# Turning x in 32x32 blocks on VectorE from a second load, in place of on TensorE, in a two-layer graph kernel

## The chip, the cores and the metric

One core of one Trainium2 chip. The time is device microseconds (us) of one execution, at a granted TensorE clock of 0.995 to 0.997 in the profiled ones. Before: 3906.45 us, median of 4 runs (3906.17 to 3907.53); the execution that was profiled took 3903.31. Verdicts count from 2%.

## The reference, cut to what matters

```python
# x: (32, 512, 512) f32, adj: (512, 512) of 0 and 1, deg = adj.sum(axis=1)
mi = einsum('bkd,od->bko', x, Wi);  mj = einsum('bkd,od->bko', x, Wj)
h  = layernorm(x + deg * (mi + b) + einsum('ij,bjo->bio', adj, mj))   # layer 0
q, k, v = heads(h @ Wq.T + bq), heads(h @ Wk.T + bk), heads(h @ Wv.T + bv)   # 8 heads of 64
out = layernorm(h + (softmax(where(adj == 0, -inf, q k^T / 8)) @ v) @ Wo.T + bo)   # layer 1
```

The kernel's matmuls sum over the partitions of their operands, so layer 0 needs x turned (feature in the partition) times the degrees, called XD here, and the gathered neighbours adj x, called AX_T.

## The kernel before

A period works on three batches at once and is cut into eight attention steps. Each begins with scores and the values of the step before, followed by pieces of projections: `l0` (layer 0), `v`, `q`, `k` and `pj` (output projection). Each projection is computed in seven products by a Strassen-like scheme, so a piece is called q6, and GpSimd makes the differences that it needs (`combos`). The turn of x stood in the gather:

```python
def l0_gather(b, dc, bank, adjT=None):
    xt = XT[b]
    if dc == 0:
        XD[b] = big()
        AX_T[b] = big()
    pt = turn_tile()                                   # PSUM, of the scores' pool
    for jc in range(NC):
        nc.tensor.transpose(pt[:, jc*P:(jc+1)*P], xt[:, jc, dc*P:(dc+1)*P], ident)
    nc.vector.tensor_mul(XD[b][:, dc, :], pt, deg_r)
    pm = mm_tile(bank)
    ...                                                # adj x: 4 + 4 matmuls
    nc.scalar.copy(AX_T[b][:, dc, :], pm)
```

Which piece stands in which step is not written down: it follows from weights.

```python
STEPS = 2 * HP
PC, TR, GA = 1.73, 0.44, 1.9           # a piece, a turn, a gather
...
    g = [(TR + GA, l0_gather, n, dc, A) for dc in range(DC)]
...
def by_steps(todo):                     # equal shares of the summed weights
    total, done, at, res = sum(f[0] for f in todo), 0.0, 0, []
    for step in range(STEPS):
        res.append([])
        while at < len(todo) and (done < total * (step + 1) / STEPS - 1e-6 or step == STEPS - 1):
            res[-1].append(todo[at])
            done += todo[at][0]
            at += 1
    return res
```

## Time and profile before

| | before |
|---|---|
| time | 3906.45 us |
| TensorE busy | 3853.7 us, 99% |
| one period, first scores to first scores, mean of 27 | 120.06 us |
| first scores of the first period | 107.6 us |

The chain of waits, followed back from the last instruction:

```profile
PE 77%; DVE 12%; POOL 8%; issue 2%; ACT 1%; DMA 0%; SPq 0%
```

The chain passes through another engine wherever TensorE was released by it, however short the wait was.

### The profile page before, as it was taken

The numbers are of one execution on the slowest core, as the hardware profiler recorded it, in microseconds if no ns is written. First come the engines' busy times: TensorE is split into PE (matmuls) and PEld (weight loads), VectorE is DVE, ScalarE is ACT, GpSimd is POOL, SyncE is SP. The second block draws the span as 40 slices with busy tenths as digits, with TensorE's granted clock in tenths as the row PEclk, the third lists the DMA queues.
The fourth block names the chain that finished last, engine by engine and source line by source line (L and its number), as shares of the span: only waits on it lengthen the run. The fifth ranks groups of instructions, "written<-read, shape, count | busy, mean of one in ns | idle before, by whom it ended". The sixth has DMA issues, their size and how long they took to land.

```text
span 3901.5 us, 46958 instructions
## 1 busy us (share of the span) xinstructions
PE 3853.7 (99%) x17402; PEld 2641.4 (68%) x17402; DVE 2595.7 (67%) x3520; ACT 1057.0 (27%) x1476; POOL 1909.7 (49%) x1861
## 2 busy tenths in 40 slices
PE   9999999999999999999999999999999999999997
PEld 6666666766666666676666666666666667666663
DVE  4667676666666676666767666666667666676765
ACT  2222222222222222322222222222222232222222
POOL 4455544554544545445555455453454544555533
PEclk9999999999999999999999999999999999999998
DMA  7333333323334233343333343333433333333330
GB/s 251 116 108 100 114 108 116 120 92 110 115 108 124 87 116 111 111 119 108 99 115 108 116 119 92 109 116 108 124 87 116 111 111 119 108 99 115 108 108 23
DMA packets 281865, 433.87 MB, mean 111 GB/s; under 512 B 23072, under 2 KB 119840, under 8 KB 281632
## 3 DMA queue, kind: packets, MB, share of 16 engines
q1 hardware_dynamic: 281376, 430.27, 36.2%
q8 instruction: 142, 2.33, 0.2%
q14 instruction: 91, 0.75, 0.1%
q0 software_dynamic: 256, 0.53, 0.0%
HBM read 389.29 MB, written 41.42 MB: 110 GB/s over the span
## 4 chain that ended last, share of the span: by engine, by line
PE 77%; DVE 12%; POOL 8%; issue 2%; ACT 1%; DMA 0%; SPq 0%
PE mma L375 23%; PE mmb L375 23%; PE sc L427 10%; PE ov L448 9%; POOL xh L390 5%; PE mmb L299 3%; DVE rl L470 3%; PE mma L299 3%; PE ov L455 2%; DVE xh L393 2%; DVE st L265 2%; POOL big L344 2%; DVE e L432 2%; POOL es L438 2%; PE sc L292 2%
## 5 line engine op out<-in xcount | busy, mean ns | idle before, releaser
L432 DVE TENSOR_TENSOR e<-sc,edge 128x1024 f32<-128x1024 f32 x512 | 602.1, 1217 | 424.3 <-ACT sc L431 424.3
L431 ACT ACTIVATE sc<-sc 128x1024 f32<-128x1024 f32 x512 | 492.8, 1006 | 1271.3 <-PE sc L427 1271.1
L375 PE MATMUL mmb<-ring,big 128*128 128x256 f32 x3144 | 731.5, 381 | 3.4 <-POOL big L344 3.0
L375 PE MATMUL mma<-ring,big 128*128 128x256 f32 x3112 | 725.2, 381 | 4.2 <-POOL big L344 3.1
L375 PEld LDWEIGHTS mmb<-ring,big 128*128 128x128 f32 x3144 | 590.8, 190 | 124.1 <-DVE e L432 23.5
L375 PEld LDWEIGHTS mma<-ring,big 128*128 128x128 f32 x3112 | 583.9, 190 | 129.5 <-DVE e L432 25.2
L344 POOL TENSOR_TENSOR big<-big 128x512 f32<-128x512 f32 x376 | 549.8, 1489 | 220.1 <-DVE big L293 177.9
L184 POOL TENSOR_TENSOR xlo<-xh,xhi 128x512 fp32r<-128x512 f32 x128 | 203.1, 1597 | 735.1 <-ACT xhi L183 735.1
L427 PE MATMUL sc<-q,k 64*128 64x512 f32 x2048 | 509.5, 616 | 0.0
L448 PE MATMUL ov<-e,v 128*64 128x512 f32 x2048 | 496.0, 605 | 5.7 <-DVE oT L480 5.7
L470 DVE RECIPROCAL rl<-ov 128x128 f32<-128x128 f32 x512 | 462.6, 929 | 9.7 <-PE ov L465 5.5
L375 PE MATMUL mma<-big,ring 128*128 128x256 f32 x1808 | 433.1, 382 | 2.2 <-DVE xh L393 2.2
L375 PE MATMUL mmb<-big,ring 128*128 128x256 f32 x1776 | 425.3, 382 | 3.1 <-DVE xh L393 2.2
L267 POOL TENSOR_SCALAR mv<-mv 128x1 f32<-128x1 f32 x256 | 50.8, 198 | 735.5 <-DVE mv L266 724.1
L438 POOL TENSOR_TENSOR es<-e 128x1024 f32<-128x1024 f32 x128 | 301.4, 2355 | 198.6 <-PE ov L455 185.6
L375 PEld LDWEIGHTS mma<-big,ring 128*128 128x128 f32 x1808 | 337.9, 190 | 80.5 <-issue 26.0
L375 PEld LDWEIGHTS mmb<-big,ring 128*128 128x128 f32 x1776 | 332.0, 190 | 78.6 <-issue 24.3
L448 PEld LDWEIGHTS ov<-e,v 128*64 128x64 f32 x2048 | 124.5, 136 | 345.8 <-issue 270.9
L440 DVE TENSOR_TENSOR es<-es,e 128x1024 f32<-128x1024 f32 x248 | 341.6, 1377 | 0.0
L427 PEld LDWEIGHTS sc<-q,k 64*128 64x128 f32 x2048 | 176.5, 186 | 208.7 <-issue 208.2
L393 DVE TENSOR_TENSOR xh<-xh,mma 128x512 f32<-128x512 f32 x186 | 125.6, 676 | 213.1 <-PE mma L375 213.1
L393 DVE TENSOR_TENSOR xh<-xh,mmb 128x512 f32<-128x512 f32 x186 | 125.7, 676 | 203.6 <-PE mmb L375 202.5
(145 smaller groups left out, 3812.4 us busy)
## 6 DMA issues: line engine op xcount, KB each, us to landing
ring<-wq SPq DMA_DIRECT2D x160, 256.0 KB, 2.6
ring<-wv SPq DMA_DIRECT2D x160, 256.0 KB, 2.6
ring<-wk SPq DMA_DIRECT2D x160, 256.0 KB, 5.4
ring<-wi SPq DMA_DIRECT2D x155, 256.0 KB, 2.6
ring<-wj SPq DMA_DIRECT2D x155, 256.0 KB, 2.7
ring<-wo SPq DMA_DIRECT2D x155, 256.0 KB, 2.6
xh<-in_x_dram SPq DMA_DIRECT2D x32, 1024.0 KB, 6.0
out_dram<-xh SPq DMA_DIRECT2D x31, 1024.0 KB, 5.2
```

The costliest lines, as they stand in the source:

```text
L184: nc.gpsimd.tensor_sub(lo, xs, hi.bitcast(FT))
L299: nc.tensor.matmul(pm, parts[w][:, jc, :], adjR[:, jc, :], start=(w == 0 and jc == 0), stop=(w == 1 and jc == NC - 1))
L344: nc.gpsimd.tensor_tensor(dst, p, q, op=OP.subtract)
L375: nc.tensor.matmul(pm[:, c * Q:(c + 1) * Q], lhs, rhs, start=first, stop=(kc == 1 and n == len(terms) - 1), skip_group_check=True)
L393: nc.vector.tensor_tensor(d, d, pm, op=OP.add)
L427: nc.tensor.matmul(ps[:, s, :], KT[b, hp // 2][r, hp % 2, kc * P:(kc + 1) * P], QT[b, hp // 2][r, hp % 2, :], start=True, stop=True)
L431: nc.scalar.activation(ps, ps, AF.Exp, scale=QSCALE)
L432: nc.vector.tensor_tensor(e, ps, edge[:, kc:kc + 1, :].to_broadcast([P, 2, N]), op=OP.mult)
L438: nc.gpsimd.tensor_add(ES[hp], E[0], E[1])
L440: nc.vector.tensor_add(ES[hp], ES[hp], E[half])
L448: nc.tensor.matmul(PV[hp][s * HD:(s + 1) * HD, :], V[b][:, kc, c0:c0 + HD], E[kc][:, s, :], start=(kc == 0), stop=(kc == NC - 1))
L470: nc.vector.reciprocal(rl[:, c], pl[:, c])
```

## The change

Its intent: TensorE is the bound, so take work off it. From batch 1 on a second load puts 32x32 blocks of x where they belong after the turn, each block still unturned; VectorE turns the blocks, and GpSimd multiplies by the degrees. TensorE turns only h. The tile for the second load takes 8 KB per partition, and the ring of weights gives up four tiles for it. The core of the diff (cuts are marked `...`; `z(...)` puts work into the plan with weight 0):

```diff
+    def load_xa(b, q):
+        if q == 0:
+            XA[b] = work([P, DC, N], "xa", 1)
+        src = x[b].rearrange("(t p) (c q f) -> q p c t f", p=32, q=4, f=32)
+        nc.sync.dma_start(XA[b][32*q:32*q+32].rearrange("p c (t f) -> p c t f", f=32), src[q])
...
-    RING = 12
+    RING = 8
...   # l0_gather: the turn and its multiply only for a batch that is not in XA
+    def l0_turn(b, dc):
+        if dc == 0:
+            XD[b] = big()
+        nc.vector.transpose(XD[b][:, dc, :], XA[b][:, dc, :])
+        nc.gpsimd.tensor_tensor(XD[b][:, dc, :], XD[b][:, dc, :], deg_r, op=OP.mult)
...   # phase_a(n)
-        g = [(TR + GA, l0_gather, n, dc, A) for dc in range(DC)]
+        g = [(GA, l0_gather, n, dc, A) for dc in range(DC)]
             res += g[i:i + 1] + k[i:i + 1]
+            if n + 1 < B:
+                res += [z(load_xa, n + 1, i)]
...   # phase_c(n), after the pieces q6 and v6, q7 and v7, q4 and v4, q5 and v5
+            if n + 1 < B and i != 3:
+                res += [z(l0_turn, n + 1, (6, 7, 4, 5).index(i))]
```

Batch 1's second load stands at the start, between the load of x and that of the last weights.

More of the change, by code (lines that the diff above doesn't have):

```diff
@@ L96, in turn_tile @@
         return sc_tile()[:, 0, :]
-    XT, XD, AX_T, HT, MV = {}, {}, {}, {}, {}
+    XT, XA, XD, AX_T, HT, MV = {}, {}, {}, {}, {}, {}
     QT, KT, V, OT = {}, {}, {}, {}
@@ L103, in rows @@
         return ap.rearrange("(c p) d -> p c d", p=P)
+    def load_xa(b, q):
+        if q == 0:
+            XA[b] = work([P, DC, N], "xa", 1)
+        src = x[b].rearrange("(t p) (c q f) -> q p c t f", p=32, q=4, f=32)
+        nc.sync.dma_start(XA[b][32 * q:32 * q + 32].rearrange("p c (t f) -> p c t f", f=32), src[q])
     def load_x(b):
@@ L148, in gnn_attention_kernel @@
     load_x(1)
+    for q in range(4):
+        load_xa(1, q)
     wo = load_w(work([P, NC, D], "xh", 3), woT, nc.sync)
@@ L287, in l0_gather @@
         if dc == 0:
-            XD[b] = big()
+            if b not in XA:
+                XD[b] = big()
             AX_T[b] = big()
-        pt = turn_tile()
-        for jc in range(NC):
-            nc.tensor.transpose(pt[:, jc * P:(jc + 1) * P], xt[:, jc, dc * P:(dc + 1) * P], ident)
-        nc.vector.tensor_mul(XD[b][:, dc, :], pt, deg_r)
+        if b not in XA:
+            pt = turn_tile()
+            for jc in range(NC):
+                nc.tensor.transpose(pt[:, jc * P:(jc + 1) * P], xt[:, jc, dc * P:(dc + 1) * P], ident)
+            nc.vector.tensor_mul(XD[b][:, dc, :], pt, deg_r)
         pm = mm_tile(bank)
@@ L307, in l0_gather @@
             split(b, dc + 2)
+    def l0_turn(b, dc):
+        if dc == 0:
+            XD[b] = big()
+        nc.vector.transpose(XD[b][:, dc, :], XA[b][:, dc, :])
+        nc.gpsimd.tensor_tensor(XD[b][:, dc, :], XD[b][:, dc, :], deg_r, op=OP.mult)
     def base(b, half):
```

## The prediction

> **What bounds the kernel now.** I read the page's busy table first, then TensorE's own waits, then the turns of x one by one in the timeline.
>
> ```profile
> span 3901.5 us, 46958 instructions
> PE 3853.7 (99%) x17402; PEld 2641.4 (68%) x17402; DVE 2595.7 (67%) x3520; ACT 1057.0 (27%) x1476; POOL 1909.7 (49%) x1861
> ```
>
> TensorE is idle for 3901.5 - 3853.7 = 48 us in all, at a granted clock of 0.997. The ends of matmuls are modelled, so 99% alone proves little. The list of what TensorE waited for is the better witness:
>
> ```profile
> PE ov L448 <- DVE oT L480: 5.7, 4, 2.5
> ...
> PE mma L375 <- POOL big L344: 3.1, 14, 0.2
> PE mmb L375 <- POOL big L344: 3.0, 14, 0.2
> PE mma L375 <- DVE xh L393: 3.0, 15, 0.8
> PE mmb L375 <- DVE xh L393: 2.2, 14, 0.2
> ```
>
> (Us in total, times, longest.) All its waits come to 36 us, and the first of these lines and those left out stand almost wholly in the first 10 us or the last 165. In the 31 periods between it waits some 12 us. So in steady state the end is set by how much TensorE has to issue, and time comes off only where TensorE's own work goes, or is lost where another engine newly makes it wait. (The chain of waits gives VectorE 12% and GpSimd 8%; I don't take that as removable, since TensorE hardly idles for them.)
>
> Now the work to be removed, the turns of x:
>
> ```profile
> L292 PE MATMUL sc<-ident,xh x512: 272/273/331, 14.4 to 3684.6; 128*128 128x128 f32 x171
> ...
> 1142.40 0.60 PE L292 MATMUL sc<-ident,xh 128*128 128x128 f32 x4
> 1142.76 1.17 PE L299 MATMUL mma<-adjR,xhi 128*128 128x512 f32 x4
> ...
> 1163.15 0.66 PE L292 MATMUL sc<-ident,xh 128*128 128x128 f32 x4
> 1163.56 1.17 PE L299 MATMUL mma<-adjR,xhi 128*128 128x512 f32 x4
> ```
>
> One turn reads as 273 ns, and four as 0.60 us, but matmuls overlap: the next work starts 0.36 us after the first of four (1142.40 to 1142.76), or 0.41 us where the turn follows an attention matmul. The start to start time is what TensorE pays, not the printed 0.60.
>
> **What the Trainium skill says.**
> - "VectorE: DVE Perf Modes", section "The three transpose paths": VectorE turns only 32x32 blocks, each by itself, and takes 311 ns for 128x128 bf16. "Vector Engine (DVE) Microarchitecture Reference", section 3.8, has the turn sustain one element per cycle per lane. The kernel before has no such instruction; its 128x512 one-source conversion from PSUM took 0.69 us (L163). Scaling 311 ns by 384 more elements at 0.96 GHz (the first page's clock) gives 0.71 us. I take 0.70 as an estimate, 0.62 from start to start, as neighbours of that length show.
> - "SBUF — State Buffer", section "Who interferes with whom": a VectorE instruction with two SBUF inputs and a GpSimd one that reads SBUF block each other. The trace agrees: the sums of exponentials (L440, two SBUF inputs) take 1218 ns at the median and up to 2175.
> - "DMA: Bandwidth & Descriptors", section "Specifications": pieces under 512 B miss the line rate. The second load moves 128 B pieces. The trace has 48 such packets, at 13 to 44 ns each.
>
> **The change part by part.** A period (one batch) is 125 us, 31 of them lose their turns (batch 0 keeps its own).
>
> 1. *TensorE loses 31 x 4 groups of four turns.* In the period shown they cost 0.36 + 0.36 + 0.35 + 0.41 = 1.48 us. 31 x 1.48 = 45.9 us. This lies wholly on the bounding engine. Ideal result: 3906.7 - 45.9 = 3861.
>
> 2. *VectorE: multiply out of PSUM replaced by a turn in SBUF.* 124 x 0.68 us (L293) go, 124 x 0.70 come: about 0 in sum. But the work moves, from the gathers to between the last pieces of q and v. There VectorE's evictions have deadlines of one or two pieces (1.73 us each). The timeline of VectorE in that stretch, before:
>
> ```profile
> 1135.69 0.69 DVE L401 TENSOR_TENSOR v<-mmb,p 128x512 f32<-128x512 f32 x1 [1.24 <-PE mmb L375]
> 1136.30 1.22 DVE L440 TENSOR_TENSOR es<-es,e 128x1024 f32<-128x1024 f32 x1
> 1137.43 0.87 DVE L418 SCALAR_TENSOR_TENSOR q<-mma,bq_c,q 128x256 f32<-128x256 f32 x2
> 1138.22 1.51 DVE L440 TENSOR_TENSOR es<-es,e 128x1024 f32<-128x1024 f32 x1
> 1139.65 0.68 DVE L403 TENSOR_TENSOR v<-v,mmb 128x512 f32<-128x512 f32 x1
> 1140.88 0.88 DVE L418 SCALAR_TENSOR_TENSOR q<-mma,bq_c,q 128x256 f32<-128x256 f32 x2 [0.55 <-PE mma L375]
> ```
>
> No idle time for 4.6 us, and then only 0.55. The plan also drops 4 x 0.44 from a period's weights, so attention steps begin elsewhere. By the kernel's rule I get for the fifth step: scores, values, q4, v4, q5, v5, q3, v3 (before: v4, q5, v5, q3, v3 and a gather), with turns after the scores, after v4 and after v5. Counted from the step's start with the trace's durations: q4 leaves TensorE at 5.57 and is evicted by 6.53, the first sum of exponentials runs to 7.67, v4's eviction to 8.28, the second sum to 9.70, the turn to 10.33, and q5's eviction to about 11.2. TensorE wants that bank for q3 at 10.75. So about 0.45 us of new waiting in a period, 30 x 0.45 = 14 us. The other three turns fall on slack by the same counting.
>
> 3. *The moved steps give something back.* Before, the first step ends with a projection that waits for GpSimd's differences (the 3.1 + 3.0 us of such waits listed for banks a and b, about 0.2 us a period). Now scores and values come between. Minus 6 us.
>
> 4. *GpSimd gains 124 multiplies* of 128x512 with two SBUF inputs, the form of L344, median 1272 ns: 158 us, 49% to about 53% busy. It has the room, but block and be blocked by VectorE's two-input sums just in the tight stretch of point 2; I put 4 us on it. In exchange the differences of x need no longer wait for VectorE (178 us of GpSimd's idle time end with L293); that idle time costs TensorE nothing today, so I count nothing.
>
> 5. *DMA gains 1 MB a period in 8192 pieces.* At 16 to 44 ns on 16 engines that is 8192 / 16 x 16 to 44 ns = 8 to 23 us of DMA time, 2 to 6 us for each of the four loads. DMA is now 36% busy over a period, so about 43 to 55% after. Hidden, unless it holds up the weights.
>
> 6. *The ring of 8 in place of 12.* Weights now land far ahead:
>
> ```profile
> ring<-wq SPq DMA_DIRECT2D x160, 256.0 KB, 2.6
> xh<-in_x_dram SPq DMA_DIRECT2D x32, 1024.0 KB, 6.0
> ...
> SPq L486 <- ACT xh L272: 155.4, 31, 54.7
> ```
>
> I set every tile's landing against its first matmul: at least 17 us, median 26, are between. Four tiles less are some 10 us less; issuing each tile when the eighth before it is released, behind the same stores and loads of x in the queue, I get at least 8 us. So nothing is lost, if each new load keeps the queues for less than about 7 us (55 ns a packet).
>
> 7. *Start.* 1 MB more of small pieces stands ahead of the last weights; first needed at 53 us, they were issued at 15 us. I put 3 us on stores behind them.
>
> Sum: -45.9 + 14 - 6 + 4 + 3 = -31 us, 3876. I lean to the lighter side, since the waiting of point 2 hangs on a few tenths, and say **3871 us**, 0.9% less.
>
> **The rivals.**
> - *The whole 46 us arrive (3858 to 3862).* For it: TensorE hardly waits today, VectorE has a third of its time free, XD is ready much earlier. Against it: the tight stretch above. Perhaps three in ten.
> - *VectorE becomes the bound locally.* If the turn takes twice my estimate (1.4 us), the wait before q3 grows to about 1.2 us and others appear before v3 and v7: 1.5 us a period, the gain is cancelled, 3900 to 3910. For it: no 32-bit turn was measured here. One in ten.
> - *The ring starves.* If 128 B packets take over 55 ns, four loads of over 7 us run into a ring that lost a third of its depth. At 62 ns (8 us) the sum of the shortfalls is small, at 80 ns it would be 30 us or more a period at worst, and the kernel clearly slower, over 4000. For it: the skill's warning on pieces under 512 B. Against it: 15 ns is the commonest of the trace's few 128 B packets, and 1 KB takes 46. Under one in ten.
> - *The gain is larger than the turns' own time.* It would need TensorE to have other waits worth taking; the list has too few. 2% is 78 us; the turns and the waits of the periods together are 46 + 12 = 58.
>
> **Range and chances.** 3855 is all of point 1 and 3 with nothing lost; 3893 is 14 us left of the gain. Faster by over 2% (under 3829) 0.02, within 2% 0.93, slower by over 2% 0.05, nearly all of it from the ring.
>
> **What would show it.** TensorE's busy time should fall by about 45 us with its turns of x at 16 (batch 0); VectorE's turns should read about 0.7 us; GpSimd should be near 53%; a wait of TensorE on VectorE's evictions of q (about 0.45 us before q3, some 14 us in all) should appear and the wait on GpSimd's differences should go. Tiles of the ring should wait for their loads nowhere. Wrong would be: TensorE waiting for DMA, loads of the second copy landing after 8 us or more, a turn well over 1 us, or a time under 3850 (then TensorE paid more for a turn than starts show).

## The result, and the profile after

The changed kernel took **3837.43 us** (median of 4, 3835.97 to 3838.15): 69 us less. The ratio is 0.9822, 95% interval 0.9805 to 0.9839. Ratios are the mean time of one kernel's fast runs over that of the other's of the same rounds, so not quite the ratio of the medians. The prediction was wrong: 3871 was said and 3855 was its low end, and the gain of 69 us is nearly twice the 36 forecast.

The page and its chain of waits, after:

```profile
span 3835.8 us, 46277 instructions
PE 3794.4 (99%) x16906; PEld 2595.5 (68%) x16906; DVE 2587.3 (67%) x3520; ACT 1064.0 (28%) x1476; POOL 1990.0 (52%) x1985
...
q1 hardware_dynamic: 537312, 462.78, 41.7%
...
PE 92%; DVE 5%; ACT 1%; DMA 1%; issue 1%; POOL 0%; SPq 0%; POOLq 0%; DVEq 0%; ACTq 0%
```

TensorE's busy time fell by 59 us, not by the 46 of the turns. GpSimd left the chain (8% to 0%) although it works more. DMA engines are 42% busy in place of 36%. TensorE's waits after (line waited for, us in total, times, longest):

```profile
PE ov L466 <- DVE oT L498: 5.8, 5, 2.5
PE sc L169 <- DVE big L163: 5.4, 3, 4.0
...
PE mma L393 <- ACT p L400: 3.0, 1, 3.0
PE mma L310 <- POOL xlo L193: 1.5, 1, 1.5
PE mma L393 <- DVE v L419: 1.1, 2, 0.6
```

Nothing that recurs every period is left in the list, and no load is in it. What the moved work costs, by its own lines (shortest, median and longest in ns; first start to last end in us). VectorE's turn:

```profile
L324 DVE STREAM_TRANSPOSE big<-xa x124: 651/702/707, 76.2 to 3597.5; 128x512 f32<-128x512 f32 x124
```

GpSimd's multiply:

```profile
L325 POOL TENSOR_TENSOR big<-big,deg_r x124: 1261/1269/1282, 77.1 to 3598.2; 128x512 f32<-128x512 f32 x124
```

The second load, among the page's DMA issues (KB each, median us from issue to landing):

```profile
xa<-in_x_dram SPq DMA_DIRECT2D x124, 256.0 KB, 3.8
```

Turn 702 ns, multiply 1269 ns, load 3.8 us from issue to landing, all near the estimates. The error is elsewhere. To find it I measured every piece of work on TensorE from its first matmul's start to the start of what follows, and averaged over 28 periods of each kernel. These sums are mine, from the records of the trace; a period went from 120.05 to 117.65 us:

| place in the period | before | after | difference |
|---|---|---|---|
| four groups of turns of x | 1.48 | 0 | -1.48 |
| pj2 (second product of the output projection) | 2.12 | 1.78 | -0.34 |
| l06 and pj6 (with the wait at pj6) | 5.76 | 5.38 | -0.38 |
| gathers and pieces beside them: g0, k6, g1, k7, g2, g3 | 11.36 | 11.05 | -0.31 |
| v5 and q3 (with the wait at q3) | 3.50 | 3.75 | +0.26 |
| the rest, mostly borders of steps | | | -0.15 |

A piece without a wait takes 1.73 us, one of `l0` 3.46. Much of what counts stands in the list of waits in part or not at all, for that list counts idle time only from the modelled end of the matmul before. At pj6 it had 0.21 us; from start to start l06 took 3.83 us in place of 3.46. TensorE at that place before, then after (start, busy time from first to last, engine, line, operation, output and inputs, forms, count, and in brackets the idle time before it):

```profile
1062.43 2.29 PE L375 MATMUL mma<-ring,oT 128*128 128x256 f32 x8
1064.56 3.62 PE L375 MATMUL mmb<-ring,big 128*128 128x256 f32 x16
1068.39 1.99 PE L375 MATMUL mma<-ring,big 128*128 128x256 f32 x8 [0.21 <-POOL big L344]
1070.32 1.99 PE L427 MATMUL sc<-q,k 64*128 64x512 f32 x8
```

```profile
1050.48 1.94 PE L393 MATMUL mma<-ring,oT 128*128 128x256 f32 x8
1052.25 3.62 PE L393 MATMUL mmb<-ring,big 128*128 128x256 f32 x16
1055.80 1.99 PE L445 MATMUL sc<-q,k 64*128 64x512 f32 x8
1057.72 1.94 PE L466 MATMUL ov<-e,v 128*64 128x512 f32 x8
1059.58 2.00 PE L393 MATMUL mma<-ring,big 128*128 128x256 f32 x8
```

Compare starts. pj2 (first line) lasted 2.13 and now 1.77 us, without any wait being printed in either. l06 lasted 3.83 before pj6 could begin; after, scores and values (`sc`, `ov`) come between.

### The profile page after: what moved, and what is told of

The parts are those of the page before. It is cut to its first block, busy times and chain, and to the rows that moved or that the text cites. A ratio compares the mean times of both kernels' runs of the same rounds, so it can differ in the third digit from the quotient of the medians.

```text
span 3835.8 us, 46277 instructions
## 1 busy us (share of the span) xinstructions
PE 3794.4 (99%) x16906; PEld 2595.5 (68%) x16906; DVE 2587.3 (67%) x3520; ACT 1064.0 (28%) x1476; POOL 1990.0 (52%) x1985
## 3 DMA queue, kind: packets, MB, share of 16 engines
q8 instruction: 138, 2.26, 0.2%
## 4 chain that ended last, share of the span: by engine, by line
PE 92%; DVE 5%; ACT 1%; DMA 1%; issue 1%; POOL 0%; SPq 0%; POOLq 0%; DVEq 0%; ACTq 0%
PE mmb L393 29%; PE mma L393 29%; PE sc L445 12%; PE ov L466 11%; PE mmb L310 3%; PE mma L310 3%; PE ov L473 3%; DVE e L450 2%; PE sc L338 1%; DVE st L274 1%; DVE es L458 1%; ACT sc L449 1%; DVE rl L488 1%; DVE xh L411 0%; DVE mv L275 0%
## 5 line engine op out<-in xcount | busy, mean ns | idle before, releaser
L362 POOL TENSOR_TENSOR big<-big 128x512 f32<-128x512 f32 x376 | 524.8, 1424 | 205.7 <-ACT big L316 165.0
L325 POOL TENSOR_TENSOR big<-big,deg_r 128x512 f32<-128x512 f32 x124 | 157.4, 1269 | 512.4 <-DVE big L324 512.4
L458 DVE TENSOR_TENSOR es<-es,e 128x1024 f32<-128x1024 f32 x248 | 319.5, 1288 | 0.0
L193 POOL TENSOR_TENSOR xlo<-xh,xhi 128x512 fp32r<-128x512 f32 x128 | 163.4, 1287 | 213.3 <-ACT xhi L192 213.3
L408 POOL TENSOR_TENSOR xh<-xh,p 128x512 f32<-128x512 f32 x186 | 231.8, 1273 | 45.8 <-ACT sc L449 39.0
```

Of the source, the lines that this page charges most:

```text
L193: nc.gpsimd.tensor_sub(lo, xs, hi.bitcast(FT))
L362: nc.gpsimd.tensor_tensor(dst, p, q, op=OP.subtract)
L408: nc.gpsimd.tensor_tensor(d, d, p1, op=OP.add)
L458: nc.vector.tensor_add(ES[hp], ES[hp], E[half])
```

## The experiments

All were correct unless said. Two questions: what of the 69 us comes from the plan's new borders, and what from work moved off the gathers? "Period" is measured as above.

### The old plan with the new turns, and the new plan with the old turns

```diff
# the changed kernel
-        g = [(GA, l0_gather, n, dc, A) for dc in range(DC)]
+        g = [(TR + GA, l0_gather, n, dc, A) for dc in range(DC)]
```

> The changed kernel with the weight of a turn (0.44) put back into the plan, so that attention steps begin where they began before; everything else as changed. Theory A (part of the gain beyond the turns comes from where the steps now begin: scores and values stand between l0 piece 6 and projection piece 6, which waited 0.38 us for GpSimd before): that wait returns, the period grows by 0.3 to 0.4 us, the time is 3846 to 3850. The wait in projection piece 2 stays gone. Rival B (the extra gain comes from VectorE's and GpSimd's work moving out of the gathers): within 3 us of the changed kernel, 3835 to 3840.

```diff
# the kernel before
-        g = [(TR + GA, l0_gather, n, dc, A) for dc in range(DC)]
+        g = [(GA, l0_gather, n, dc, A) for dc in range(DC)]
```

> The kernel before with only the plan's weight of a gather lowered by 0.44, turns still on TensorE. Theory A: the wait before projection piece 6 goes, 0.3 to 0.4 us a period, the time falls to 3893 to 3898; projection piece 2 keeps its wait of 0.34 us. Rival B: 3904 to 3908.

Measured: the old plan with the new turns 3880.84 us (ratio to before 0.9935, 0.9921 to 0.9948), the new plan with the old turns 3888.25 us (0.9953, 0.9939 to 0.9967). Before was 3906.43 in these rounds. So the weights alone, not one instruction removed, are worth 18 us; the turns alone 26 us; both together 69. The first is 31 us above the range expected and the second 5 below; theory A's direction held, and rival B, that the plan counts for nothing, fell.

They do more than add up. With the old plan the wait at pj6 returned as expected (l06 3.84 us), but two new ones came: q3 grew from 1.77 to 2.27 us, and the first gather from 2.02 to 2.70. The waits of TensorE in that run:

```profile
PE mma L310 <- POOL xlo L193: 5.6, 15, 1.6
PE mmb L310 <- POOL xlo L193: 4.3, 15, 0.3
...
PE mma L393 <- DVE v L421: 4.1, 15, 0.3
PE mmb L393 <- DVE v L421: 3.9, 14, 0.3
```

And GpSimd and TensorE at that place, same run:

```profile
1137.45 1.27 POOL L325 TENSOR_TENSOR big<-big,deg_r 128x512 f32<-128x512 f32 x1 [2.38 <-DVE big L324]
1138.67 2.52 POOL L193 TENSOR_TENSOR xlo<-xh,xhi 128x512 fp32r<-128x512 f32 x2
```

```profile
1138.44 1.29 PE L310 MATMUL mma<-adjR,xhi 128*128 128x512 f32 x4
1140.01 1.18 PE L310 MATMUL mma<-adjR,xlo 128*128 128x512 f32 x4 [0.28 <-POOL xlo L193]
```

The gather needs the low part of x (`xlo`), which GpSimd makes after the multiply of the last turn. With the old plan the gather follows v3 directly and meets it unfinished; with the new one, scores, values and sums (4.64 us) stand between. The first gather takes 1.95 us after, and 1.93 in the new plan with the old turns. Here pj2 stayed at 1.78 us with the new turns and at 2.13 with the old ones, whichever plan, so that part is not the plan's.

### The turn put back at the gather

VectorE's turn and GpSimd's multiply stand ahead of each gather, the second load where the turns were.

```diff
-            res += g[i:i + 1] + k[i:i + 1]
-            if n + 1 < B:
-                res += [z(load_xa, n + 1, i)]
+            res += [z(l0_turn, n, i)] + g[i:i + 1] + k[i:i + 1]
...
-            if n + 1 < B and i != 3:
-                res += [z(l0_turn, n + 1, (6, 7, 4, 5).index(i))]
+            if 0 < n < B - 1 and i != 3:
+                res += [z(load_xa, n + 1, (6, 7, 4, 5).index(i))]
```

> The changed kernel with VectorE's turn and GpSimd's multiply put where the multiply stood before, just ahead of each gather, and the second load moved to the turns' old places; plan of the changed kernel. Theory A2 (projection piece 2 no longer waits because the differences of x on GpSimd start earlier and block VectorE's two-input work less): with 4 multiplies of 1.27 us added to GpSimd in that stretch its wait returns or grows, 0.3 to 0.8 us a period, 3847 to 3862. If only the removal of the turns from TensorE matters: 3835 to 3840.

Measured: 3846.30 us (0.9848, 0.9834 to 0.9861), just under the low end of what was expected. pj2 takes 2.40 us, 0.62 more than in the changed kernel; q3 waits no more, which gives 0.3 back. VectorE, then GpSimd, ahead of pj2 in this run, then in the kernel before, then in the changed one:

```profile
1154.37 6.78 DVE L330 SCALAR_TENSOR_TENSOR xh<-b_r,deg_c,xh 128x512 f32<-128x512 f32 x4
...
1167.53 0.69 DVE L498 TENSOR_TENSOR oT<-ov,rl 128x512 f32<-128x512 f32 x1
...
1152.09 10.19 POOL L362 TENSOR_TENSOR big<-big 128x512 f32<-128x512 f32 x6
```

```profile
1048.23 2.12 DVE L440 TENSOR_TENSOR es<-es,e 128x1024 f32<-128x1024 f32 x1
1050.27 5.77 DVE L312 SCALAR_TENSOR_TENSOR xh<-b_r,deg_c,xh 128x512 f32<-128x512 f32 x4
...
1062.41 0.69 DVE L480 TENSOR_TENSOR oT<-ov,rl 128x512 f32<-128x512 f32 x1
...
1044.70 10.13 POOL L344 TENSOR_TENSOR big<-big 128x512 f32<-128x512 f32 x6 [6.00 <-DVE big L293]
```

```profile
1036.27 1.78 DVE L458 TENSOR_TENSOR es<-es,e 128x1024 f32<-128x1024 f32 x1
1037.98 5.75 DVE L330 SCALAR_TENSOR_TENSOR xh<-b_r,deg_c,xh 128x512 f32<-128x512 f32 x4
...
1050.11 0.69 DVE L498 TENSOR_TENSOR oT<-ov,rl 128x512 f32<-128x512 f32 x1
...
1034.47 8.04 POOL L362 TENSOR_TENSOR big<-big 128x512 f32<-128x512 f32 x5 [5.68 <-ACT big L316]
```

pj2 waits for `oT`, the scaled attention output. Ahead of it in VectorE's queue stand a sum of exponentials (1.22 us when alone) and four additions of the bias (0.74 us the shortest seen, 3 us together), all with two inputs in SBUF, and GpSimd makes its differences beside them. Against the period's first scores those differences end at +2.32 us before, +1.97 after, +4.95 here, and `oT` is ready at +10.60, +10.25 and +10.90. So in the kernel before, GpSimd began late because it waited for VectorE's multiply of the last turned column (178 us in all), and its lateness came back to TensorE through VectorE: the sum takes 2.12 us before and 1.78 after, which is the whole 0.35 us, while the four additions take 5.77 and 5.75. In this run the sum takes 1.40 and the additions 6.78. And in the second period of the kernel before (from 213 us) the differences end before the additions begin: there an addition takes 0.74 us, and pj2 1.73. The changed kernel has XD ready a phase earlier. The order of cause is shown from both sides (gone with the turns moved, under both plans; back when GpSimd gets work there); that the blocking is that of a shared SBUF port is what the Trainium skill says ("SBUF — State Buffer", section "Who interferes with whom"), and these durations fit it.

### The ring alone

```diff
# the kernel before
-    RING = 12
+    RING = 8
```

> The kernel before with the ring of weights cut from 12 to 8 tiles, nothing else. My prediction's count leaves 8 us between landing and use, so nothing changes: 3905 to 3909. A rival in which the ring's depth matters (loads further ahead or behind others in the queue) would show over 3915 or, if a shorter ring made queues shorter, under 3900.

Measured: 3904.99 us (0.9996, 0.9981 to 1.0011). No effect, as expected.

### The turn done twice

```diff
-        nc.vector.transpose(XD[b][:, dc, :], XA[b][:, dc, :])
+        for _ in range(2):
+            nc.vector.transpose(XD[b][:, dc, :], XA[b][:, dc, :])
```

> The changed kernel with each of VectorE's turns done twice (same result). Theory (VectorE's slack in the new plan is small only ahead of q5's eviction): about 0.6 us a period more, nearly all in q3's wait, 3850 to 3860. Rival (VectorE is 67% busy, so another 124 x 0.65 us hide): 3836 to 3840.

Measured: 3878.15 us (0.9932, 0.9917 to 0.9947): 41 us more and 18 above the range, but wholly at the place named: the period grew by 1.29 us where 0.6 was expected, all of it before q3. VectorE there:

```profile
1131.76 1.45 DVE L325 STREAM_TRANSPOSE big<-xa 128x512 f32<-128x512 f32 x2
1133.13 0.83 DVE L437 SCALAR_TENSOR_TENSOR q<-mma,bq_c,p 128x256 f32<-128x256 f32 x2
1133.88 1.76 DVE L459 TENSOR_TENSOR es<-es,e 128x1024 f32<-128x1024 f32 x1
```

The longer turn itself fits into idle time. But it makes GpSimd's multiply start later, into the sum of exponentials, which takes 1.76 us in place of 1.22. That is 0.54 us; the doubled turn of column 2 gives the other 0.7.

### The second load made once, and a ring of 6

```diff
     def load_xa(b, q):
+        if b > 1:
+            XA[b] = XA[1]
+            return
```

> The changed kernel with the second load of x made once, for batch 1, and its tile used for all later batches: wrong results on purpose, 120 loads of 256 KB in 128 B pieces fewer. Theory (the small pieces are hidden wholly behind TensorE): 3834 to 3840, the same period of 117.65 us. Rival (they delay the weights or x): under 3830.

Measured: 3836.44 us (0.9822, 0.9807 to 0.9837), with a wrong result; a period is 117.64 us. The changed kernel moves 254,000 packets of 128 B; leaving out 120 of the 124 loads saves no time that can be seen beside TensorE.

The next is the changed kernel with `RING = 6`.

> The changed kernel with a ring of 6 in place of 8. From loads that landed in 2.6 to 2.8 us and the second load's 3.8 us, some 4 us remain between landing and use at the tightest: 3836 to 3842. Rival (8 was already at the edge): over 3850.

Measured: 3838.87 us (0.9826, 0.9810 to 0.9841). Two tiles more could be given away.

### Batch 1's load later, and two turns after v3

```diff
-    for q in range(4):
-        load_xa(1, q)
...   # first(): z(load_xa, 1, q) for q = 0..3 between the later steps of batch 0
...
-            if n + 1 < B and i != 3:
-                res += [z(l0_turn, n + 1, (6, 7, 4, 5).index(i))]
+            if n + 1 < B:
+                res += [z(l0_turn, n + 1, dc) for dc in {6: (0,), 7: (1,), 3: (2, 3)}.get(i, ())]
```

> The changed kernel with batch 1's second load spread over the first batch's steps in place of all at the start, and the turns of columns 2 and 3 after v3 in place of v4 and v5. Theory: the start gives back 3 us (first scores at 108 in place of 111 us) and the wait before q3 goes (0.2 us a period, 6 us): 3826 to 3831. If turns after v3 delay the next step's scores instead: 3835 or more.

Measured: 3834.18 us (0.9818, 0.9805 to 0.9832), between the two ranges. The start came back (first scores at 107.2 us; 110.8 and 109.5 in the two profiles of the changed kernel). The wait before q3 went in 19 of the 29 periods counted (v5 and q3 1.73 us each). In the other 10 it was larger than before (v5 2.26 to 2.42 us), though no turn stands ahead of q5's eviction any more. (The profile is of the fastest of the five executions, 3831.26 us.) VectorE and then GpSimd in one of these 10:

```profile
1115.46 1.22 DVE L456 TENSOR_TENSOR es<-es,e 128x1024 f32<-128x1024 f32 x1
1116.60 0.68 DVE L417 TENSOR_TENSOR v<-mmb,p 128x512 f32<-128x512 f32 x1
1117.20 2.26 DVE L456 TENSOR_TENSOR es<-es,e 128x1024 f32<-128x1024 f32 x1
```

```profile
1117.10 3.48 POOL L191 TENSOR_TENSOR xlo<-xh,xhi 128x512 fp32r<-128x512 f32 x2 [1.71 <-ACT xhi L190]
```

With the multiplies of columns 2 and 3 out of its way, GpSimd's split of x started 0.1 us ahead of the second sum, and the sum took 2.26 us, 1.04 more. The sum begins at the same place of its step in all 29 periods, the split does not. Where the split began at least 0.04 us ahead of it (10 periods), the sum took 2.15 to 2.31 us and the first of the two instructions of the split 1.27; where it began later than that (19), the sum took 1.21 or 1.22, and the first instruction of the split up to 2.38. So one waits for the other, and a few hundredths of a us decide which. One delay left, and in a third of the periods another took its place.

### The turn of column 2 after q5

```diff
+                if i == 5 and f[2] == "q" and n + 1 < B:
+                    res += [z(l0_turn, n + 1, 2)]
...
-            if n + 1 < B and i != 3:
+            if n + 1 < B and i in (6, 7, 5):
```

The start is as in the run before; the turn of column 2 now stands behind q5's eviction, and GpSimd's split still behind its multiplies.

> The changed kernel with batch 1's second load spread over the first batch's steps and the turn of column 2 right after q5's piece in place of after v4's, so that q5's eviction stands ahead of it on VectorE; the other turns stay. Theory: the start gives back 3.5 us and the wait before q3 (0.2 to 0.25 us a period) goes without the sums of exponentials running into GpSimd's splits as in the last run: 3825 to 3830, v5 back to 1.73 us. If another collision takes its place: 3832 to 3836.

Measured: **3826.54 us** (3825.49 to 3826.93; 0.9797, 0.9784 to 0.9810), within what was expected. It beats both kernels: the changed one, run again beside it, took 3837.06 (3835.52 to 3837.53). VectorE there:

```profile
1118.18 1.22 DVE L456 TENSOR_TENSOR es<-es,e 128x1024 f32<-128x1024 f32 x1
1119.32 0.87 DVE L434 SCALAR_TENSOR_TENSOR q<-mma,bq_c,q 128x256 f32<-128x256 f32 x2
1120.10 0.70 DVE L322 STREAM_TRANSPOSE big<-xa 128x512 f32<-128x512 f32 x1
```

The sum is unblocked, the eviction follows at once, the turn comes third. v5 fell from 1.92 to 1.73 us and q3 from 1.83 to 1.73.

### The multiply on VectorE, and the changed kernel again

```diff
-        nc.gpsimd.tensor_tensor(XD[b][:, dc, :], XD[b][:, dc, :], deg_r, op=OP.mult)
+        nc.vector.tensor_tensor(XD[b][:, dc, :], XD[b][:, dc, :], deg_r, op=OP.mult)
```

> The changed kernel with the multiply by the degrees after each turn on VectorE in place of GpSimd (0.69 in place of 1.27 us). Theory (VectorE's queue between q4 and q3 is what is tight, GpSimd has room): column 1's multiply fits in VectorE's idle 0.63 us, column 2's adds some 0.65 us to the wait before q3: 3853 to 3862. Rival (taking 158 us off GpSimd frees VectorE's two-input work): 3830 to 3840.

Measured: 3890.31 us (0.9958, 0.9943 to 0.9973): 53 us slower than the changed kernel, 28 beyond the range. The wait stands where it was named: v5 takes 3.48 us on average, 1.92 in the changed kernel. In 2 of 29 periods GpSimd's split came late and v5 took 2.69: 0.77 more, about one multiply (0.69), as expected. In the other 27 VectorE stood beside the splits, which GpSimd reaches early when it has no multiplies: the sum took 1.88 to 2.29 us in 13 of them, and in the rest v5 took 3.01 to 3.55 (in the two of these that were looked at, the multiply took 1.02 and 1.47). So, by this count, about half of what v5 grew by is the work moved and about half the blocking. Taking work off GpSimd slowed VectorE's own.

> The changed kernel unaltered, on the chip of these runs, as their measure: 3836 to 3839.

Measured: 3837.06 us (0.9823, 0.9810 to 0.9837), the measure for the two above.

## Why the prediction was wrong, point by point

The bound was named rightly, and the size was wrong by half. By its own steps:

1. *Turns off TensorE, 45.9 us.* Right: 1.48 us a period are gone. Beside the gathers another 0.12 us a period came with them (from the new plan with the old turns to the changed kernel: k6 and k7 0.19 us each less, the gathers 0.26 more in sum); why, no run shows.
2. *VectorE's turn, 14 us of new waiting before q3.* Place right, size too large: v5 and q3 grew by 0.24 us against the same plan with the old turns, some 7 us in all. The turn took 0.70 us as estimated; I had q5's eviction done at 11.2 us of its step (the "fifth", counted from zero), and it was done about 0.25 us earlier.
3. *"The moved steps give something back", minus 6 us.* The largest error: measured by itself it is 18 us. I took 0.2 us from the list of waits, which starts at the modelled end of a matmul. From start to start pj6 alone waited 0.38 us, and other borders gave the rest. What I did not see at all is that the plan also keeps the new turns from harm: under the old one they would have gained 26 us.
4. *GpSimd's 124 multiplies, plus 4 us, and its earlier differences "I count nothing".* Wrong in sign. The list of idle times named the 178 us that GpSimd waited for VectorE, and I dismissed them since TensorE did not wait for GpSimd there. It waited one step further on, at pj2, by way of VectorE: 0.35 us a period, some 10 us. Nor did the multiplies add what they take: they are 157 us, but GpSimd's busy time rose by 80 (1909.7 to 1990.0). By my sums over the records, its splits of x took 40 us less in all, its differences 24 and its normalisation 13 less, and VectorE's sums of exponentials 22 less, as fits two engines that block each other less often.
5. *DMA hidden*: right. The packets of 128 B took 13 ns.
6. *The ring costs nothing*: right; 8 alone changes nothing, and 6 does not either.
7. *Start, 3 us*: right in direction, the size is not settled. The first scores stand 3.2 us later in these two profiles, but 1.9 later in the second profile of the changed kernel (109.5), and with the ring alone they stood at 109.1.

Against the steps as predicted, that is 12 us in point 3, 14 in point 4, 7 in point 2 and about 4 in point 1: 37 us on top of the 31 of its sum, near the 69 measured. (The prediction also gave the period as 125 us, where it is 120.06; its sum does not rest on that.) So the step that failed is how waits were valued: points 3 and 4 took them from the list of waits and found 6 us and nothing, where the runs showed 18 and 10. Of the rivals, "the gain is larger than the turns' own time" is what happened; it was dismissed by adding up the same list of waits. "A time under 3850 (then TensorE paid more for a turn than starts show)" drew the wrong conclusion in advance: starts showed it rightly for the turns, I had just not used them for anything else.

## What to carry to other kernels

On an engine that seems 99% busy, measure each piece of work from start to start and compare it with its own shortest time; waits of 0.2 to 0.4 us that recur every period hide behind modelled ends and the two largest were worth some 10 us each here (0.35 and 0.38 us, 30 times). When a plan is built from weights, changing a weight is a change of its own: run it alone. And ask of an engine that is not the bound not how busy it is but what its work will stand beside: here GpSimd's start decided whether a sum on VectorE took 1.22 us or over 2.1, and giving GpSimd's multiply to VectorE cost 53 us, in part by such blocking.

## What the Trainium skill lacked or had wrong

- "VectorE: DVE Perf Modes", section "The three transpose paths", gives VectorE's turn for 128x128 bf16 alone. Here 128x512 in 32 bits took 702 ns at the median (651 to 707). One element per cycle per lane, as the "Vector Engine (DVE) Microarchitecture Reference", section 3.8, has it, would by estimate be 533 ns at the 0.96 GHz of the first page, so the figure does not contradict it; what the rest is was not measured. No page has the 32-bit figure.
- "TensorE: Matmul & The Clock Gate", section "Part 4: PE-mode transpose", gives about 275 ns for a bf16 turn in one kernel. The records here say 273 ns for f32, but four in a row delay what follows by only 0.36 us. The section lacks the cost of turns in a stream, which is what removing one saves; the spacing in a stream that the page gives elsewhere is for other matmuls.
- "DMA: Bandwidth & Descriptors", section "Specifications", warns of pieces under 512 B, and the page has no time for a load from HBM in pieces of 128 B. Here 256 KB in such pieces landed after 3.8 us, where 256 KB in rows of 2 KB took 2.6 to 2.8, and a packet of 128 B took 13 ns.
- "SBUF — State Buffer", section "Who interferes with whom", fits: a two-input sum of 1.22 us took 2.26 when GpSimd's split began 0.1 us ahead of it (two instructions, 3.48 us here and 2.52 in another run). The page says that issue order decides, and that run fits it in 27 of 29 periods; in the other two the starts lie under 0.04 us apart. It lacks the consequence seen here, that GpSimd's work done earlier, or taken off it, can slow VectorE.
